# VectorE without two-SBUF-input and copy-mode operations from the first group on; gate rows spread by DMA; split tokens laid by feature chunk; order planned anew

## The chip, the cores and the metric

The kernel runs on one core of one Trainium2 chip, with fp32 inputs. The metric is the device time of one launch in microseconds, as the median of several runs; a profiled execution is taken beside them. PE is TensorE, DVE is VectorE, ACT is ScalarE, POOL is GpSimd and SP is SyncE, which here only issues DMAs. POOL issues DMAs too.

## The reference

One transformer block with adaptive layer norms. `x` has 8 batches of 1024 tokens and 512 features; the six modulation rows of a batch come from `silu(c) @ wmod`.

```python
x = L0_attn_x                                   # 8, 1024, 512
mod = (_silu(L0_c) @ L0_wmod).reshape(8, 6, 1, -1)
sa, ca, ga, sb, cb, gb = (mod[:, i] for i in range(6))
ga = (2 * (ga >= 0) - 1) * jnp.maximum(jnp.abs(ga), 0.25)      # gb likewise
h = _layernorm(x) * (1 + ca) + sa
x = x + ga * attn(h)
h = _layernorm(x) * (1 + cb) + sb
x = x + gb * ffn(h)

# attn: xn = _ln(h, lna_w); q, k, v = projections, 16 heads of 32 features
for it in range(3):
    ql, kl, vl = qcur[:, :, :16] @ Wlq.T + blq, kcur[:, :, :16] @ Wlk.T + blk, vcur[:, :, :16] @ Wlv.T + blv
    t_it = temp0 + 0.005 * it
    tscale = where((t_it != 1.0) & (t_it > 0), rsqrt(t_it), 1.0)
    qs, ks_ = _ln(ql, lnc_w) * tscale, _ln(kl, lnd_w)
    ai = softmax(qs @ ks_.T * sm_scale) @ vl
    iter_out = zeros_like(qcur).at[:, :, :16].set(ai)          # only the first 16 tokens
    diff = mean(abs(iter_out - prev))
    attn_out = where(done, attn_out, iter_out)
    done = done | (diff < thr + fac * diff) & (it > 0)
    prev, qcur, kcur, vcur = iter_out, qcur + iter_out, kl, vl
attn = attn_out @ Wo.T + bo

# ffn: tokens and weight quantized to a 6-bit grid in blocks of 32 features, scale = max(|block|) / 7.5
out = dequantized(x) @ dequantized(weight).T + bias
```

Attention reaches only the first 16 tokens of each batch. For all others `attn` is the row `bo`, so the block's first half adds one gate row `ga * bo` per batch.

## The kernel before

**Groups.** The 1008 tokens per batch outside attention make two groups, one of 4 x 128 and one of 4 x 124 tokens: 16 groups for 8 batches. The 128 attention tokens (16 of each batch) form one tile `xs` of 128 x 512, whose work is spread between the groups from group 2 on.

**One group.** `load(g)`, three groups ahead, brings the tokens with the gate row `ga * bo` added: in mode P SP loads `x` and POOL adds the row `g2B` to each of four tiles (three tiles of group 0 are added on DVE); in mode A ACT copies the row into the tile four times and POOL issues a DMA that adds the tokens to it. `front(g)` normalizes: ACT takes sum and sum of squares with `accum_out`, `rsqrt` runs over ACT, DVE and POOL, and DVE applies two three-operand steps per tile (`A` and `B_`, the modulation rows spread over the partitions, lie in PSUM). DVE reduces the maximum of each block of 32 features (`M`), scales it, and takes the reciprocal `I`. POOL multiplies each tile by `I` into an fp8 tile `q8`, which rounds to the grid, and back by `M` into `x`. PE transposes the tile to `psT`; ACT copies it to `xh` in the reduced format of fp32 that PE multiplies faster, and DVE keeps the remainder `xl = psT - xh`. `back(g)` makes each of four output chunks from 12 matmuls (`xh*wh`, `xh*wl`, `xl*wh`, four feature chunks each) in `psO`; ACT evicts with scale `gbT` and bias `cbT`, POOL issues a DMA that adds the transposed tokens `xT`, and SP stores `outT`. Groups 0 and 1 are cut into parts, the last group is evicted on DVE.

**Gate rows.** `rows(name, src)` takes a 128 x 4 x 8 gate (features on the partitions), writes a negated and a remainder half into `hl`, transposes both and copies 40 rows to SBUF. A matmul with the selector `sel` then spreads a row over the partitions: `make_g2(b)` for the row `g2B` of batch b (copied by ACT from `psT`), `row_s` for RGA and RGB, the gates of the attention tile.

**Attention.** `attc` prepares constants: the two weight matrices centred by their block means (`m2`, `bdc`), the centred biases `rcf`, and the temperature factors `wct`. Three iterations alternate `mix`, `norm`, 32 x 32 transposes, 128 small matmuls for the logits, softmax and 128 small matmuls for the result. After the second, `ds` and `dm` hold whether the iteration had converged; they choose between `ai[1]` and `ai[2]`. Then come the output projection, the gate RGA, the second normalization, quantization, 12 matmuls, the gate RGB and the store `outS`.

**Order.** Every instruction is recorded with a cost and issued in an order that `Program.issue` plans: a list schedule over all engines, whose priorities come from due times per strand (`DUE`, scaled by `LAM`, `MU`, `LAMD`) and from the windows `WP`, `WV`, `WS`, `WE`, `WG` within which an engine is held for a more urgent instruction. The planner has a model of the exclusion between DVE and POOL: `locks` names the instructions concerned, and a locked one starts only when the other engine's current locked instruction is over. Dependences come from `_region`, the span of a tile that an access covers. On the chip each engine, and SP's and POOL's DMA queues, run in exactly the planned order. All instructions are issued through one helper, so that the profile gives them all line 206 and they are told apart by their tiles.

Of the kernel before, what the change touches and what calls it, by code (L numbers as in the profile page):

```python
# [27 lines left out]
LAM = {"gpsimd": 3.714, "scalar": 2.438, "sync": 1.213, "tensor": 0.799, "vector": 5.221}  # L28
MU = 708.0
LAMD = 3.212  # L30
# [3 lines left out]
    "w3": 75770.0,  # L34
    "gb": -217233.0,
    "mod": -252945.0,
    "L0": -248576.0,
    "B0.0": 53715.0,
    "B0.1": 39421.0,
    "B0.2": 59671.0,  # L40
    "B0.3": 62459.0,
    "Q1": -146914.0,
    "B1.0": 75209.0,
    "B1.1": 78188.0,
    "B1.2": 81166.0,
    "B1.3": 84553.0,
    "att0": 32581.0,
    "kv0": 44759.0,
    "it0": 56937.0,
    "kv1": 69216.0,  # L50
    "it1": 81393.0,
    "kv2": 93571.0,
    "it2": 105748.0,
    "end": 152949.0,
    "end2": 165127.0,
    "F2": -150662.0,
    "B2.0": 90191.0,
    "B2.1": 93169.0,
    "B2.2": 96915.0,
    "B2.3": 99126.0,  # L60
    "B3.0": 102005.0,
    "B3.1": 110387.0,
    "B3.2": 107962.0,
    "B3.3": 108731.0,
    "B4.0": 115098.0,
    "B4.1": 118077.0,
    "B4.2": 118615.0,
    "B4.3": 124034.0,
    "B5.0": 123238.0,
    "B5.1": 131709.0,  # L70
    "B5.2": 134688.0,
    "B5.3": 137666.0,
    "L9": -32519.0,
    "B6.0": 142024.0,
    "B6.1": 143731.0,
    "B6.2": 147981.0,
    "B6.3": 150376.0,
    "B7.0": 155080.0,
    "B7.1": 158058.0,
    "B7.2": 154929.0,  # L80
    "B7.3": 164015.0,
    "Q8": 39438.0,
    "B8.0": 168254.0,
    "B8.2": 174211.0,
    "B8.3": 177189.0,
    "F9": 34764.0,
    "B9.0": 162035.0,
    "B9.1": 165249.0,
    "B9.2": 167992.0,
    "B9.3": 172508.0,  # L90
    "B10.0": 193959.0,
    "B10.1": 197581.0,
    "B10.2": 200560.0,
    "B10.3": 203538.0,
    "Q11": 118602.0,
    "B11.0": 207787.0,
    "B11.1": 210766.0,
    "B11.2": 213744.0,
    "B11.3": 216723.0,
    "B12.0": 220952.0,  # L100
    "B12.1": 223986.0,
    "B12.2": 226909.0,
    "B12.3": 229887.0,
    "F13": 142459.0,
    "Q13": 170365.0,
    "B13.0": 234126.0,
    "B13.1": 237105.0,
    "B13.2": 240083.0,
    "B13.3": 243061.0,
    "B14.0": 246786.0,  # L110
    "B14.1": 248083.0,
    "B14.2": 252743.0,
    "B14.3": 255722.0,
    "Q15": 251792.0,
    "B15.0": 260600.0,
    "B15.1": 252121.0,
    "B15.2": 266084.0,
    "B15.3": 269410.0,
# [30 lines left out]
def _region(ap):  # L149

    dims = [tuple(d) for d in ap.ap]
    if ap.space == PSUM:
        return ap.tensor.name, 0, P, 0, 1 << 30
    w = 1
    for s in ap.tensor.shape[1:]:
        w *= s
    p0, f0 = divmod(ap.offset, w)
    np_ = dims[0][1]
    f1 = f0 + sum((n - 1) * abs(s) for s, n in dims[1:]) + 1
    return ap.tensor.name, p0, p0 + np_, f0, f1  # L160
# [9 lines left out]
class Program:  # L170
# [22 lines left out]
    def record(self, name, eng, meth, args, kw):  # L193
# [16 lines left out]
        for ap, wr in [(r, False) for r in reads] + [(w, True) for w in writes]:  # L210
            if ap.space == bass.MemoryType.DRAM:
                continue
            t, a, b, c, d = _region(ap)
            hist = self.acc.get(t, [])
            keep = []
            for h in hist:
                j, w, a2, b2, c2, d2 = h
                over = a < b2 and a2 < b and c < d2 and c2 < d
                if over and (w or wr) and j != i:
                    deps.add(j)  # L220
                if not (wr and a <= a2 and b2 <= b and c <= c2 and d2 <= d):
                    keep.append(h)
            keep.append((i, wr, a, b, c, d))
            self.acc[t] = keep
# [200 lines left out]
def _adaln(ctx: ExitStack, tc: tile.TileContext, t):  # L425
# [11 lines left out]
    WP = 2821  # L437
    WV = 402
    WS = 1017
    WE = 1637  # L440
    WG = 8296
# [27 lines left out]
    xhr = Ring("xh", 2, [P, 4, 4, P], F32R)  # L469
    xlr = Ring("xl", 2, [P, 4, 4, P], F32R)  # L470
# [51 lines left out]
    pkb = new("pkb", [P, 661])  # L522
# [162 lines left out]
    hl = Ring("hl", 2, [P, 4, 40], F32R)  # L685
    for z in hl.tiles:
        G.memset(z.bitcast(F32), 0.0)

    def rows(name, src):

        w = hl()
        V.tensor_scalar(w[:, :, 0:NB], src, -1.0, None, ALU.mult)
        V.scalar_tensor_tensor(w[:, :, 32:40], src, -1.0, w[:, :, 0:NB], ALU.mult, ALU.subtract)
        w = w.bitcast(F32)
        ps = psX()
        for c in range(4):
            PE.transpose(ps[:40, c * P : (c + 1) * P], w[:, c], ident)
        r = new(name, [40, D], F32R)
        S.copy(r, ps[:40])
        return r  # L700

# [13 lines left out]
    def make_g2(b):  # L715
        ps = g2P[b] = psT()
        if b:
            PE.matmul(ps, lhsT=sel[:40, b, :], rhs=Rg2, start=True, stop=True)
        else:
            for c in range(4):  # L720
                PE.matmul(
                    ps[:, c * P : (c + 1) * P],
                    lhsT=g2T[:, c, 0:1].broadcast_to([P, P]),
                    rhs=ident,
                    start=True,
                    stop=True,
                )
        z = g2r()
        S.copy(z, ps)
        g2B[b] = z  # L730
# [3 lines left out]
    Rg2 = rows("Rg2", g2T)  # L734
# [14 lines left out]
    V.tensor_tensor(cbT, gbT, cb(1), ALU.mult)  # L749
    V.tensor_tensor(cbT, cbT, g2T, ALU.add)  # L750
# [52 lines left out]

    def front(g, parts):
# [6 lines left out]
        for js in parts:  # L811
# [30 lines left out]
            V.tensor_scalar(M[:n, : 16 * m], M[:n, : 16 * m], 64.0 / 7.5, 64e-30, ALU.mult, ALU.max)  # L842
            V.reciprocal(I[:n, : 16 * m], M[:n, : 16 * m])
            prog.strand = (g + 1, f"Q{g}")
            for j in js:
# [10 lines left out]
                S.copy(xh[:, j, :, :n], pv)  # L856
                V.tensor_tensor(xl[:, j, :, :n], pv, xh[:, j, :, :n], ALU.subtract)
        return xh, xl

    def back(g, xh, xl, last=False):  # L860
# [14 lines left out]
        for o, j0, m in pieces:  # L875
# [4 lines left out]
            for xs, ws in ((xh, wh), (xh, wl), (xl, wh)):  # L880
                for c in range(4):
                    PE.matmul(ps[:, :M], lhsT=ws[:, o, c, :], rhs=xs[:, j0 : j0 + m, c, :n], start=(i == 0), stop=(i == 11))
# [14 lines left out]
    def attention():  # L897
# [4 lines left out]
        cols, v32, sc = pkb[:, 0:12], pkb[:, 12:18], pkb[:, 18:21]  # L902
        bd = b3(pkb[:, 21:405], P)
        bmask, wk = pkb[:, 405:533], pkb[:, 533:661]
# [17 lines left out]
        V.tensor_scalar(cols[:, 0:4], cols[:, 0:4], qk, None, ALU.mult)  # L922
        V.tensor_scalar(cols[:, 8:12], cols[:, 8:12], -0.5, None, ALU.mult)

        bdc = new("bdc", [P, 2, P])
        m2 = new("m2", [P, 2])
        V.tensor_reduce(m2, bd[:, 0:2], AX.X, ALU.add)
        V.tensor_scalar(m2, m2, 1.0 / 32, None, ALU.mult)
        for i in range(2):
            V.scalar_tensor_tensor(bdc[:, i], bd[:, i], m2[:, i : i + 1], bmask, ALU.subtract, ALU.mult)  # L930
        ps = psX()
        PE.matmul(ps[:, 0:2], lhsT=bmask, rhs=v32[:, 4:6], start=True, stop=True)
        rcf = new("rcf", [P, 2])
        V.scalar_tensor_tensor(rcf, ps[:, 0:2], -1.0 / 32, v32[:, 4:6], ALU.mult, ALU.add)
# [12 lines left out]
        V.scalar_tensor_tensor(wcd, v32[:, 2:3], 0.25, v32[:, 3:4], ALU.mult, ALU.mult)  # L947
# [3 lines left out]
        for i in range(3):  # L951
            V.tensor_scalar(tt[:, i : i + 1], sc[:, 0:1], 0.005 * i, None, ALU.add)
        V.tensor_scalar(tc1, tt, 1.0, None, ALU.not_equal)
        V.scalar_tensor_tensor(tc1, tt, 0.0, tc1, ALU.is_gt, ALU.mult)
        V.tensor_scalar(tt, tt, 1e-30, None, ALU.max)
        rr = rsqrt(tt, P, 3, "t")
        V.scalar_tensor_tensor(tsc, rr, -0.5, tc1, ALU.mult, ALU.mult)
        V.tensor_scalar(tc1, tc1, -1.0, 1.0, ALU.mult, ALU.add)
        V.tensor_tensor(tsc, tsc, tc1, ALU.add)
        V.tensor_scalar(wct, tsc, wcd, None, ALU.mult)  # L960
# [7 lines left out]
        V.tensor_scalar(h1, h1, nm, r, ALU.add, ALU.mult)  # L968
# [82 lines left out]
        ds, dm = new("ds", [P, 1]), new("dm", [P, 1])  # L1051
        qcur = att["WqT"]
        qflat = qcur.rearrange("p a b -> p (a b)")
        for it in range(3):
# [38 lines left out]
            for i0 in range(0, 16, 16 // PARTS):  # L1093
                with prog.together():
                    for i in range(i0, i0 + 16 // PARTS):
                        for h in range(4):
# [8 lines left out]
                            )  # L1105
            a = air()
# [4 lines left out]
            if it == 1:  # L1111
# [6 lines left out]
                V.tensor_scalar(dm, ps[:, 0:1], 1.0 / (NB * 16 * T * 32), None, ALU.mult)  # L1118
                V.scalar_tensor_tensor(ds, dm, sc[:, 2:3], sc[:, 1:2], ALU.mult, ALU.add)
                V.tensor_tensor(dm, dm, ds, ALU.is_lt)  # L1120
                V.tensor_scalar(ds, dm, -1.0, 1.0, ALU.mult, ALU.add)
        prog.strand = ("end", "end")
        V.tensor_scalar(ai[2], ai[2], ds, None, ALU.mult)
        V.scalar_tensor_tensor(ai[2], ai[1], dm, ai[2], ALU.mult, ALU.add)
# [8 lines left out]
        for c in range(4):  # L1133
            PE.matmul(ps, lhsT=ai[2][:, c * P : (c + 1) * P], rhs=w[:, c], start=(c == 0), stop=(c == 3))
        V.tensor_tensor(h1, ps, boP, ALU.add)
        V.tensor_tensor(h1, h1, row_s(rows("RGA", gaT)), ALU.mult)
# [8 lines left out]
        V.tensor_scalar(M, M, 64.0 / 7.5, 64e-30, ALU.mult, ALU.max)  # L1145
# [116 lines left out]
```

## Time and profile before

| | |
|---|---|
| median of 3 runs | 312.61 us (311.56 to 313.08) |
| profiled execution | 310.64 us, its span 308.9 us |
| mean granted PE clock in it | 0.955 |
| DMA | 63.22 MB, mean 205 GB/s |
| POOL's DMA queue | 25.99 MB, 44.8% of the 16 engines' time |
| SP's DMA queue | 36.84 MB, 31.4% |

The busiest groups of each engine, as the page gives them (operation, tile, count, total us, mean ns):

| engine | group | count | us | mean ns |
|---|---|---|---|---|
| PE | MATMUL psO<-xh,wh | 292 | 101.8 | 393 |
| PE | MATMUL psT<-pka,x | 256 | 56.4 | 281 |
| POOL | x<-q,s_M | 64 | 71.9 | 1204 |
| POOL | q<-x,s_I | 64 | 70.3 | 1149 |
| DVE | x<-x,s_nm,psA | 64 | 44.9 | 731 |
| DVE | s_M<-x (maximum) | 19 | 36.8 | 1938 |
| ACT | y<-psO,cbT,gbT | 68 | 49.1 | 723 |
| ACT | x<-g2B | 40 | 22.5 | 625 |

A row's mean is the length of one instruction as the profiler saw it. Matmuls overlap their neighbours, so that the distance between their starts is shorter than their length. A line of a timeline has the start, the length of the merged instructions, engine, operation, output and inputs; what stands in brackets is the idle time before it and the instruction that ended it. The line of 40 digits has one digit for each fortieth of the span, the busy share in tenths; the line PEclk has the granted clock in the same way.

### The profile page before, as it was taken

The numbers are of one execution on the slowest core, as the hardware profiler recorded it, in microseconds if no ns is written. First come the engines' busy times: TensorE is split into PE (matmuls) and PEld (weight loads), VectorE is DVE, ScalarE is ACT, GpSimd is POOL, SyncE is SP. The second block draws the span as 40 slices with busy tenths as digits, with TensorE's granted clock in tenths as the row PEclk, the third lists the DMA queues.
The fourth block names the chain that finished last, engine by engine and source line by source line (L and its number), as shares of the span: only waits on it lengthen the run. The fifth ranks groups of instructions, "written<-read, shape, count | busy, mean of one in ns | idle before, by whom it ended". The sixth has DMA issues, their size and how long they took to land.

```text
span 308.9 us, 6174 instructions
## 1 busy us (share of the span) xinstructions
PE 282.9 (92%) x2235; PEld 216.2 (70%) x2235; DVE 247.2 (80%) x415; ACT 236.6 (77%) x542; POOL 235.4 (76%) x352
## 2 busy tenths in 40 slices
PE   6764999999999999999999995499999999999993
PEld 2332488899797877777778774376788777887783
DVE  6899979998979976968898899959599959961312
ACT  4189889999998998999998979169599979333500
POOL 2779876799998889996999997374999986888010
PEclk9795799999999999999999999589999999999999
DMA  7999947199798697559896829459877977575777
GB/s 247 365 409 388 277 115 232 17 213 209 257 187 261 163 223 180 189 93 230 270 207 186 236 38 213 155 151 191 239 134 261 186 227 138 174 181 129 212 135 270
DMA packets 14846, 63.22 MB, mean 205 GB/s; under 512 B 1630, under 2 KB 2398, under 8 KB 10848
## 3 DMA queue, kind: packets, MB, share of 16 engines
q0 software_dynamic: 3632, 25.99, 44.8%
q1 hardware_dynamic: 11184, 36.84, 31.4%
q8 instruction: 17, 0.28, 0.3%
q14 instruction: 13, 0.11, 0.1%
HBM read 46.05 MB, written 16.78 MB: 203 GB/s over the span
## 4 chain that ended last, share of the span: by engine, by line
PE 57%; DVE 23%; POOL 9%; ACT 5%; issue 3%; DMA 1%; POOLq 0%; DVEq 0%
PE psO L206 39%; PE psX L206 10%; PE psT L206 8%; DVE x L206 7%; DVE s_M L206 5%; POOL x L206 3%; DVE dm L206 3%; POOL q L206 2%; DVE xl L206 2%; ACT jk L206 2%; ACT xh L206 1%; POOL s_u_m L206 1%; PE psA L206 1%; ACT L206 1%; POOL y L206 1%
## 5 line engine op out<-in xcount | busy, mean ns | idle before, releaser
L206 PE MATMUL psO<-xh,wh 128*128 128x512 f32 (+3 forms) x292 | 101.8, 393 | 0.5 <-ACT xh L206 0.5
L206 PE MATMUL psO<-xl,wh 128*128 128x512 f32 (+3 forms) x292 | 99.4, 384 | 0.0
L206 PE MATMUL psO<-xh,wl 128*128 128x512 f32 (+3 forms) x292 | 99.2, 401 | 0.0
L206 POOL TENSOR_TENSOR q<-x,s_I 128x512 fp8e4<-128x512 f32 (+1 forms) x64 | 70.3, 1149 | 16.8 <-DVE s_I L206 5.7
L206 POOL TENSOR_TENSOR x<-q,s_M 128x512 f32<-128x512 fp8e4 (+1 forms) x64 | 71.9, 1204 | 0.1
L206 ACT ACTIVATE y<-psO,cbT,gbT 128x512 f32<-128x512 f32 (+3 forms) x68 | 49.1, 723 | 25.3 <-PE psO L206 25.2
L206 PEld LDWEIGHTS psO<-xh,wh 128*128 128x128 f32 x292 | 53.3, 191 | 17.0 <-ACT xh L206 3.0
L206 PE MATMUL psT<-pka,x 128*128 128x128 f32 (+1 forms) x256 | 56.4, 281 | 8.6 <-DVE xl L206 7.8
L206 PEld LDWEIGHTS psO<-xh,wl 128*128 128x128 f32 x292 | 53.3, 191 | 12.9 <-issue 4.3
L206 PEld LDWEIGHTS psO<-xl,wh 128*128 128x128 f32 x292 | 53.3, 189 | 8.6 <-issue 1.0
L206 DVE TENSOR_TENSOR xl<-psT,xh 128x512 fp32r<-128x512 f32 (+1 forms) x64 | 40.9, 671 | 15.5 <-ACT xh L206 15.5
L206 DVE SCALAR_TENSOR_TENSOR x<-x,s_r_m,psB 128x512 f32<-128x512 f32 (+1 forms) x64 | 43.5, 740 | 10.1 <-POOL s_r_m L206 10.1
L206 DVE SCALAR_TENSOR_TENSOR x<-x,s_nm,psA 128x512 f32<-128x512 f32 (+1 forms) x64 | 44.9, 731 | 5.2 <-PE psA L206 3.5
L206 PEld LDWEIGHTS psT<-pka,x 128*128 128x128 f32 (+1 forms) x256 | 35.2, 145 | 18.1 <-issue 9.9
L206 ACT ACTIVATE jk<-x,s_nm 128x512 bf16<-128x512 f32 (+1 forms) x64 | 46.2, 721 | 0.6
L206 ACT CAST xh<-psT 128x512 fp32r<-128x512 f32 (+1 forms) x64 | 34.4, 577 | 12.3 <-PE psT L206 12.1
L206 ACT ACTIVATE jk<-x 124x512 bf16<-124x512 f32 (+1 forms) x61 | 38.4, 630 | 1.5 <-DMA x<-in_x 1.0
L206 DVE TENSOR_REDUCE s_M<-x 128x64 f32<-128x2048 f32 (+4 forms) x19 | 36.8, 1938 | 0.2
L206 POOL TENSOR_TENSOR x<-x,g2B 124x512 f32<-124x512 f32 (+1 forms) x21 | 27.8, 1389 | 1.7 <-DMA x<-in_x 1.7
L206 ACT COPY x<-g2B 128x512 f32<-128x512 f32 x40 | 22.5, 625 | 0.0
L206 POOL DMA_DIRECT2D y<-in_xT x15 | 13.7, 910 | 11.3 <-ACT y L206 10.9
L206 PE MATMUL psX<-ai,w 128*128 128x128 f32 x96 | 15.5, 275 | 0.0
(236 smaller groups left out, 376.8 us busy)
## 6 DMA issues: line engine op xcount, KB each, us to landing
x<-in_x POOLq DMA_DIRECT2D x10, 1024.0 KB, 10.4
y<-in_xT POOLq DMA_DIRECT2D x8, 1024.0 KB, 8.2
outT<-y SPq DMA_DIRECT2D x8, 1024.0 KB, 7.3
y<-in_xT POOLq DMA_DIRECT2D x7, 992.0 KB, 7.9
outT<-y SPq DMA_DIRECT2D x7, 992.0 KB, 4.1
x<-in_x SPq DMA_DIRECT2D x5, 1024.0 KB, 6.9
y<-in_wmod SPq DMA_DIRECT2D x16, 256.0 KB, 5.9
x<-in_wmod SPq DMA_DIRECT2D x8, 256.0 KB, 7.3
```

Source lines behind the costliest of these rows:

```text
L206: o.fn = lambda: getattr(eng, meth)(*args, **kw)
```

## The change

Four things change together.

1. From the first group on, DVE has no more instructions that read two SBUF operands or that run from SBUF to SBUF as a scaling or a copy. They go to POOL (the scaling of `M`, `cbT`, the constants of attention, two products with RGA and RGB), to ACT (the normalized `h1`, and the product of `ai[1]` with `dm`), to PE (the centred weights), or read one operand from PSUM (`dm`, `ds`, the last choice between the iterations). Three tiles of group 0 are still added on DVE.
2. `rows` writes 8 plain fp32 rows. `make_g2(b)` for b > 0 and the gates RGA and RGB of the attention tile are spread by DMAs on SP's queue instead of matmuls.
3. For groups 2 to 15 `xh` and `xl` are laid out with the feature chunk outermost and the group's 4n tokens in one run; groups 0 and 1 keep one block per tile of 128 tokens. `_region` learns of the columns within a period of 512.
4. The planner's due times and weights are other ones, so the order of all instructions is another.

The diff, with the two tables of due times left out and repeated renamings shortened:

```diff
-LAM = {"gpsimd": 3.714, "scalar": 2.438, "sync": 1.213, "tensor": 0.799, "vector": 5.221}
-MU = 708.0
-LAMD = 3.212
+LAM = {"gpsimd": 3.429, "scalar": 3.529, "sync": 0.785, "tensor": 0.578, "vector": 5.271}
+MU = 650.1
+LAMD = 2.969
...
-    WP = 2821
-    WV = 402
-    WS = 1017
-    WE = 1637
-    WG = 8296
+    WP = 4984
+    WV = 0
+    WS = 223
+    WE = 189
+    WG = 24984
...
-    xhr = Ring("xh", 2, [P, 4, 4, P], F32R)
-    xlr = Ring("xl", 2, [P, 4, 4, P], F32R)
+    xhr = Ring("xh", 2, [P, 4 * D], F32R)
+    xlr = Ring("xl", 2, [P, 4 * D], F32R)
...
-    def rows(name, src):
-
-        w = hl()
-        V.tensor_scalar(w[:, :, 0:NB], src, -1.0, None, ALU.mult)
-        V.scalar_tensor_tensor(w[:, :, 32:40], src, -1.0, w[:, :, 0:NB], ALU.mult, ALU.subtract)
-        w = w.bitcast(F32)
+    rw = new("rw", [96, D])
+
+    def rows(i, src):
+        r = rw[32 * i : 32 * i + NB]
         ps = psX()
         for c in range(4):
-            PE.transpose(ps[:40, c * P : (c + 1) * P], w[:, c], ident)
-        r = new(name, [40, D], F32R)
-        S.copy(r, ps[:40])
+            PE.transpose(ps[:NB, c * P : (c + 1) * P], src[:, c], ident)
+        S.copy(r, ps[:NB])
         return r
+
+    def spread(r, z):
+
+        for b in range(NB):
+            SY.dma_start(z[16 * b : 16 * b + 16], r[b : b + 1].unsqueeze(1).broadcast_to([1, 16, D]))
+        return z
...
     def make_g2(b):
+        z = g2B[b] = g2r()
+        if b:
+            SY.dma_start(z, Rg2[b : b + 1].unsqueeze(1).broadcast_to([1, P, D]))
+            return
         ps = g2P[b] = psT()
-        if b:
-            PE.matmul(ps, lhsT=sel[:40, b, :], rhs=Rg2, start=True, stop=True)
...
-    V.tensor_tensor(cbT, gbT, cb(1), ALU.mult)
-    V.tensor_tensor(cbT, cbT, g2T, ALU.add)
+    G.tensor_tensor(cbT, gbT, cb(1), ALU.mult)
+    G.tensor_tensor(cbT, cbT, g2T, ALU.add)
...
+    def by_tile(z, g):
+        return z.rearrange("p (j c k) -> p j c k", j=4, c=4)
+
+    def by_chunk(z, g):
+        n = GR[g][2]
+        return z.rearrange("p (c k) -> p c k", c=4)[:, :, : 4 * n]
+
+    def part(z, g, j):
+        n = GR[g][2]
+        return by_tile(z, g)[:, j, :, :n] if g < 2 else by_chunk(z, g)[:, :, j * n : j * n + n]
+
+    def moving(z, g, c, j0, m):
+        n = GR[g][2]
+        return by_tile(z, g)[:, j0 : j0 + m, c, :n] if g < 2 else by_chunk(z, g)[:, c, j0 * n : (j0 + m) * n]
...
-            V.tensor_scalar(M[:n, : 16 * m], M[:n, : 16 * m], 64.0 / 7.5, 64e-30, ALU.mult, ALU.max)
+            G.tensor_scalar(M[:n, : 16 * m], M[:n, : 16 * m], 64.0 / 7.5, 64e-30, ALU.mult, ALU.max)
...
-                S.copy(xh[:, j, :, :n], pv)
-                V.tensor_tensor(xl[:, j, :, :n], pv, xh[:, j, :, :n], ALU.subtract)
+                h, l = part(xh, g, j), part(xl, g, j)
+                S.copy(h, pv)
+                V.tensor_tensor(l, pv, h, ALU.subtract)
...
-                    PE.matmul(ps[:, :M], lhsT=ws[:, o, c, :], rhs=xs[:, j0 : j0 + m, c, :n], start=(i == 0), stop=(i == 11))
+                    PE.matmul(ps[:, :M], lhsT=ws[:, o, c, :], rhs=moving(xs, g, c, j0, m), start=(i == 0), stop=(i == 11))
...
-        V.tensor_reduce(m2, bd[:, 0:2], AX.X, ALU.add)
-        V.tensor_scalar(m2, m2, 1.0 / 32, None, ALU.mult)
-        for i in range(2):
-            V.scalar_tensor_tensor(bdc[:, i], bd[:, i], m2[:, i : i + 1], bmask, ALU.subtract, ALU.mult)
+        bdf = new("bdc", [P, 2 * P + 2])
+        bdc, rcf = b3(bdf[:, : 2 * P], P), bdf[:, 2 * P :]
         ps = psX()
-        PE.matmul(ps[:, 0:2], lhsT=bmask, rhs=v32[:, 4:6], start=True, stop=True)
-        rcf = new("rcf", [P, 2])
-        V.scalar_tensor_tensor(rcf, ps[:, 0:2], -1.0 / 32, v32[:, 4:6], ALU.mult, ALU.add)
+        PE.matmul(ps[:, :P], lhsT=wq, rhs=cen, start=True, stop=True)
+        PE.matmul(ps[:, P : 2 * P], lhsT=wk, rhs=cen, start=True, stop=True)
+        PE.matmul(ps[:, 2 * P : 2 * P + 2], lhsT=cen, rhs=v32[:, 4:6], start=True, stop=True)
+        V.tensor_copy(bdf, ps[:, : 2 * P + 2])
...
-        V.tensor_scalar(h1, h1, nm, r, ALU.add, ALU.mult)
+        nr = new("nr", [P, 1])
+        G.tensor_tensor(nr, nm, r, ALU.mult)
+        S.activation(h1, h1, AF.Identity, scale=r, bias=nr)
...
+            if it == 2:
+                V.scalar_tensor_tensor(ai[1], av, ds, ai[1], ALU.mult, ALU.add)
+                break
             a = air()
             S.copy(a, av)
...
-                V.tensor_scalar(dm, ps[:, 0:1], 1.0 / (NB * 16 * T * 32), None, ALU.mult)
-                V.scalar_tensor_tensor(ds, dm, sc[:, 2:3], sc[:, 1:2], ALU.mult, ALU.add)
-                V.tensor_tensor(dm, dm, ds, ALU.is_lt)
-                V.tensor_scalar(ds, dm, -1.0, 1.0, ALU.mult, ALU.add)
+                V.tensor_scalar(ps[:, 1:2], ps[:, 0:1], 1.0 / (NB * 16 * T * 32), None, ALU.mult)
+                V.tensor_scalar(dt_, ps[:, 1:2], sc[:, 2:3], sc[:, 1:2], ALU.mult, ALU.add)
+                V.tensor_tensor(dm, ps[:, 1:2], dt_, ALU.is_lt)
+                V.tensor_tensor(ds, ps[:, 1:2], dt_, ALU.is_lt)
+                G.tensor_scalar(ds, ds, -1.0, 1.0, ALU.mult, ALU.add)
+
+                S.mul(a, a, dm)
...
-        V.tensor_scalar(ai[2], ai[2], ds, None, ALU.mult)
-        V.scalar_tensor_tensor(ai[2], ai[1], dm, ai[2], ALU.mult, ALU.add)
...
-        V.tensor_tensor(h1, h1, row_s(rows("RGA", gaT)), ALU.mult)
+        G.tensor_tensor(h1, h1, spread(rows(1, gaT), new("RGA", [P, D])), ALU.mult)
...
-        V.tensor_scalar(M, M, 64.0 / 7.5, 64e-30, ALU.mult, ALU.max)
+        G.tensor_scalar(M, M, 64.0 / 7.5, 64e-30, ALU.mult, ALU.max)
...
-        V.tensor_tensor(h1, h1, row_s(rows("RGB", gbT)), ALU.mult)
+        G.tensor_tensor(h1, h1, spread(rows(2, gbT), new("RGB", [P, D])), ALU.mult)
```

The twelve small steps that make `cols`, `wcd`, `tt`, `tsc`, `tc1` and `wct` move from DVE to POOL in the same way; the packed constants `pkb` grow from 661 to 792 columns, with the iteration offsets, the centring matrix and the transposed weights.

## The prediction

> **What bounds the kernel now.** I read the busy shares first, then the slices, then the list of waits, and last the timeline around the longest wait.
>
> ```profile
> span 308.9 us, 6174 instructions
> ...
> PE 282.9 (92%) x2235; PEld 216.2 (70%) x2235; DVE 247.2 (80%) x415; ACT 236.6 (77%) x542; POOL 235.4 (76%) x352
> ...
> PE   6764999999999999999999995499999999999993
> ...
> PEclk9795799999999999999999999589999999999999
> ```
>
> TensorE (PE) is busy in every slice but the first four, two between 185 and 201 us and the last; its granted clock drops near 200 us too. From 60 to 180 us it works 119.5 of 120 us at full clock, while the windows view gives ACT 112.6, POOL 109.5 and VectorE (DVE) 103.2: they feed PE with little to spare. So the time is PE's work, plus its idle stretches, plus what it loses at a lowered clock. The list of waits names the longest idle stretch:
>
> ```profile
> PE psT L206 <- DVE xl L206: 7.8, 2, 7.4
> ```
>
> The timelines of DVE, of POOL and of PE there:
>
> ```profile
> 181.51 0.69 DVE L206 TENSOR_TENSOR t<-psX,s_mx 128x512 f32<-128x512 f32 x1
> 182.11 8.85 DVE L206 TENSOR_TENSOR dm<-dm,ds 128x1 f32<-128x1 f32 x1
> 190.88 2.71 DVE L206 SCALAR_TENSOR_TENSOR x<-x,s_r_m,psB 128x512 f32<-128x512 f32 x4
> ```
>
> ```profile
> 184.48 1.54 POOL L206 TENSOR_TENSOR x<-x,g2B 124x512 f32<-124x512 f32 x1
> 185.71 1.14 POOL L206 DMA_DIRECT2D x<-in_x  x1
> 186.32 2.62 POOL L206 TENSOR_TENSOR q<-x,s_I 124x512 fp8e4<-124x512 f32 x2
> 188.34 2.59 POOL L206 TENSOR_TENSOR x<-q,s_M 124x512 f32<-124x512 fp8e4 x2
> 197.97 1.05 POOL L206 TENSOR_TENSOR t<-t,s_mx 128x512 f32<-128x512 f32 x1 [7.04 <-DVE s_M L206]
> ```
>
> ```profile
> 188.76 1.07 PE L206 MATMUL psO<-xl,wh 128*128 128x512 f32 x4
> 197.24 1.06 PE L206 MATMUL psT<-pka,x 124*128 124x124 f32 x4 [7.41 <-DVE xl L206]
> ```
>
> A comparison of one element per partition, with both inputs in SBUF, takes 8.85 us and ends within 0.1 us of the moment at which POOL runs out of work (188.34 + 2.59 = 190.93). Behind it in DVE's order stand the second normalization of four tiles, their maxima and two low halves `xl` that free the transposes' PSUM, so PE idles 7.41 us. The windows behind the gap (PE busy, PEld, DVE, ACT, POOL, then the granted clock):
>
> ```profile
> 195.00:200.00 5.00, 2.77 (x10) 2.31 (x11) 4.93 (x10) 1.28 (x3) 1.93 (x2) 0.50 0.29 119
> 200.00:205.00 5.00, 5.00 (x141) 3.68 (x140) 3.06 (x6) 2.15 (x3) 4.45 (x8) 0.72 0.47 164
> ```
>
> 2.77 us of work at 0.50 lose 1.4 us, 5.00 at 0.72 lose 1.4: the stall costs PE 7.4 + 2.8 = 10.2 us. Afterwards PE is busy to the end, with ACT, DVE and POOL well under full from 260 us on, so it is not won back.
>
> That this is a class of instruction and not one accident, two rows of the scale tile show:
>
> ```profile
> L206 DVE TENSOR_SCALAR s_M<-s_M x19: 132/189/1229, 26.2 to 274.6; 128x64 f32<-128x64 f32 x7, 124x64 f32<-124x64 f32 x7, 128x16 f32<-128x16 f32 x2, 124x32 f32<-124x32 f32 x2
> L206 DVE RECIPROCAL s_I<-s_M x19: 189/541/554, 27.5 to 274.8; 128x64 f32<-128x64 f32 x7, 124x64 f32<-124x64 f32 x7, 128x16 f32<-128x16 f32 x2, 124x32 f32<-124x32 f32 x2
> ```
>
> The first form stretches ninefold (132 to 1229 ns), the reciprocal of the same tile never does.
>
> [...]
>
> **The change, part by part** (against the profiled execution: 310.64 us, span 308.9).
>
> *1. The port stalls.* `dm` and its twin `ds` now read PSUM and SBUF, as the 0.69 us subtraction above does with no stretch; the 2.23 us multiplication of `ai` and the 0.75 us step behind it become one step from PSUM (about 0.74, by the 734 ns of a three-operand row with a PSUM input). All 10.2 us of PE could return. But ACT at 94% and POOL at 91% between 60 and 180 us have to feed PE without that pause, so some of it comes back as short waits. Taken: -9; bounds -10.2 and -3.
>
> *2. PE's own work.* Seven `g2B` matmuls and the two that spread RGA and RGB go (nine; the chain shows 0.44 us for the one of RGA, rows mean 498 to 539 ns): 9 x 0.44 = 4.0. New are two 128-column f32 products and a two-column one, at most 3 x 0.28 (row of 128-column transposes) = 0.8. Taken: -3; bounds -4.5 (9 x 0.5, nothing added on the path) and 0.
>
> *3. The start.* Between 14 and 47 us the chain runs through DVE, which is busy 10.0 of the 10 us from 20 on. Off DVE go `cbT` (1.72 + 0.19), two scalings of `s_M` (1.30), two of `hl` (0.53 + 1.03), and the constants' sums and centred weights (0.40 + 0.16 + 0.34 x 2); of these the chain holds about 3.7 us (1.69, 0.15, some 1.2 of the `s_M` pieces, 0.32, 0.23, 0.12). In exchange each of the first parts sends its maximum through POOL: 0.35 us (POOL's 128x16 TENSOR_SCALAR, 353 ns) plus two hand-overs of about 0.1 to 0.2 us. Two on the chain give back 1.2. Taken: -2; bounds -4 and +1 (if each stands behind one POOL product of 1.2 us more).
>
> *4. Contiguous tokens.* The moving operand of groups 2 to 15 becomes one run. The last stretch shows four-run steps of 512 columns every 0.23 us (286.15, 286.38, 286.61); a contiguous 512 product, `psA`, also takes 0.23 on the chain. Taken: 0. Bound -2: 336 products of 496 columns now also step by about 0.23, and would by proportion step by 0.222, so 6 ns each. A slower read is excluded by the contiguous row.
>
> *5. POOL's load.* Added: 20 scalings, 14 of 64 elements at about 0.4 (between 353 ns for 16 and 1202 for 512 elements) and 6 smaller ones at 0.3, two products `h1` at 1.30 (row `xs<-xs,h`), some sixteen tiny ones at 0.2 to 0.35: 5.6 + 1.8 + 2.6 + 4.5 = about 14 us, POOL 235 to 250. DVE loses about 30 us (9.0 of `s_M` and `s_sM`, 8.7, 2.2, 1.9, 2.8, 1.9 of `h1`, 3.5 of constants), ACT about 3 (seven copies of 576 ns and one of `ai` go, two near 0.7 come). Most of it lies in POOL's idle time, but a scaling on POOL now stands between DVE's reduction and DVE's reciprocal. Taken: +2; bounds 0 and the second rival.
>
> *6. Gate rows by DMA.* Seven broadcasts of 256 KB and sixteen small ones enter SP's queue, 0.33 to 0.4 us of issue each, 9 us of a queue that mostly waits. Behind a waiting broadcast on SP stand the `outT` stores that free `y`, and the `x` loads. The trace has no copy from one partition to 128. Nearest are the broadcasts of `bo` and `bias` from DRAM, 11.0 and 4.6 us to landing; loads are issued three groups ahead, and 14 groups take from about 75 us to the end, some 15 us each. Taken: 0; bounds 0 and the first rival. [...]
>
> *7. The new order.* Nothing shows what it is worth; it carries the width, 6 us to either side.
>
> Sum: -9 - 3 - 2 + 0 + 2 = -12, so 298.6. The median of the runs lies 2.0 above the profiled execution (312.61 to 310.64): 300.6, rounded to **300**. All gains at their best: -20.7, or 292 as a median, 290 with a little of part 7.
>
> **Rivals.**
> - *Late gate rows.* SP takes its queue in order and has waited up to 15.5 us for one `y` transfer; a broadcast behind it comes late. ACT then stops in the four copies `x<-g2B`, and with it the evictions of `psO`, of which PE has two. Five groups load in this way (2, 4, 6, 10, 12); at 2 us of PE each, 10 us: **310.5**. Against it: three groups of lead.
> - *POOL's queue takes the place of the lock (slower).* Place: the scaling of each group's maximum, in order on POOL behind `q` and `x` products, which run back to back. If each of 14 groups waits one product and two hand-overs that PE sees, 14 x (1.2 + 0.3) = 21 us, against gains of 14: 310.6 + 7 + 2 = **319.5**. It decides from (14 + 1.6)/14 = 1.1 us per group on. For it: POOL at 91%, and `psT` weights already wait 9.7 us on `s_M`'s products. Against it: two `xh` buffers, and DVE, 30 us lighter, reduces earlier.
> - *The stall survives elsewhere.* [...] Then only parts 2 to 5 remain, -3: **309.5**. Against it: no reduction, transpose, reciprocal or PSUM-fed form shows a stretch.
>
> **How the numbers follow.** Forecast 0.62, late rows 0.12, POOL's queue 0.16, surviving stall 0.10. A measurement of this kernel tells about 0.5% from no change, so faster is below 311.0 and slower above 314.2. Faster: 0.62, plus 0.06 of the late rows and 0.06 of the surviving stall; same: 0.07; slower: 0.16 and 0.03 of the late rows. The forecast's own range is 292 to 307; to leave no more than 2 in 10 out it reaches over both middle rivals, to 290 and 314.
>
> **What would show it.** No DVE instruction over 2.5 us after 40 us; PE without a gap over 2 us after 60 us and with the clock at 1.00 there; no PE group from `Rg`; POOL near 250 us, DVE near 217. Wrong: a new wait of DVE's reciprocal on POOL, or of ACT's copies on the broadcasts, that adds up to 10 us of idle PE; or PE slices below 9 between 60 and 280 us.

## The result: 11% slower, and the profile after

The changed kernel takes 347.27 us (346.0 to 348.33) against 312.09 us for the kernel before in the same rounds: a ratio of 1.1122 [1.1067, 1.1177]. Forecast were 300 us, 290 to 314. The direction was wrong. (Of the experiments below, the profiled execution of the one with ACT's queue was disturbed; its page is used there, its time is not.)

The first lines of the page of the changed kernel: busy time per engine, the slices, the granted clock, the DMA engines.

```profile
span 344.9 us, 6191 instructions
...
PE 287.4 (83%) x2230; PEld 220.8 (64%) x2230; DVE 223.1 (65%) x366; ACT 233.9 (68%) x536; POOL 248.4 (72%) x389
...
PE   6872989719998864999499999459999999999992
...
PEclk9875789976999896999999999959999999999998
DMA  7999999993499996298999479996749979478596
```

DVE and POOL have come out as forecast (223 for 217, 248 for 250). But PE's row of nines is now broken in five places between the first slices and the last. Idle PE is the span less its busy time: 26.0 us before (308.9 - 282.9), 57.5 now, so 31.5 of the 36.0 us are new holes. The other 4.5 are PE's own work, longer although instructions went: the mean granted clock fell from 0.955 to 0.917, and the digits of the clock are low at most of the holes or just behind them.

What the holes wait for, from the list of waits (us in all, times, longest):

```profile
PEld psO L215 <- ACT y L215: 24.4, 11, 9.0
PE psO L215 <- ACT y L215: 21.5, 7, 8.3
ACT y L215 <- DMA outT<-y: 13.0, 3, 6.0
ACT jk L215 <- DMA x<-in_x: 18.3, 4, 7.1
ACT x L215 <- DMA g2B<-rw: 2.7, 1, 2.7
```

PE waits for evictions. ACT, which makes them, waits for `outT` stores to free a `y` buffer and for loads of `x`. The gate rows themselves delay ACT by 2.7 us once. So the culprit isn't the row that comes late; it is something that makes other transfers late. The hole at 219.6 us shows what. Timelines of SP, ACT and PE:

```profile
206.16 0.48 SPq L215 DMA_DIRECT2D g2B<-rw  x1
207.44 24.04 SPq L215 DMA_DIRECT2D outT<-y  x2
```

```profile
227.06 0.78 ACT L215 ACTIVATE y<-psO,cbT,gbT 128x512 f32<-128x512 f32 x1 [5.57 <-DMA outT<-y]
```

```profile
227.89 0.80 PE L215 MATMUL psO<-xh,wh 128*128 128x512 f32 x1 [8.33 <-ACT y L215]
```

The chain of waits names the same transfer: the `outT` issued at 207.44 takes 19.52 us, where no `outT` before took over 9.5. (Such a time runs from the issue of a DMA until all its bytes have landed.)

```profile
207.44 19.52 DMA outT<-y
```

Beside it lies the broadcast issued at 206.16, which landed after 15.2 us. The view of the DMAs from 200 to 232 us, in 40 slices of 0.8 us, shows the DMA engines' busy share and what they moved:

```profile
DMA  4897997998899979987988967999999898999985
GB/s 51 102 164 164 215 276 164 195 256 174 174 236 202 148 125 72 49 28 23 28 26 23 36 115 284 425 410 272 189 248 199 189 270 183 204 256 204 194 184 122
```

From the 18th to the 22nd slice the 16 engines are busy for 70% of the time or more and move only 23 to 28 GB/s. The trace records a transfer in packets. A packet of the broadcast (2 KB, one partition's row) takes 1.08 us; the median 2 KB packet of the kernel before took 84 ns (packet times are read from the packed traces, no view lists them). One broadcast has 128 of them. The page has the sum by queue (packets, MB, share of the 16 engines' span):

```profile
q1 hardware_dynamic: 12704, 39.27, 43.8%
q0 software_dynamic: 3632, 25.99, 38.5%
```

SP's queue held the engines for 43.8% of 344.9 = 151 us; before for 31.4% of 308.9 = 97. Only 2.4 MB were added. Their landings, and what lay beside them (us to landing):

```profile
x<-in_x POOLq DMA_DIRECT2D x10, 1024.0 KB, 16.7
...
g2B<-rw SPq DMA_DIRECT2D x7, 256.0 KB, 13.0
```

Loads on POOL's own queue went from 10.4 to 16.7 us, so it is not SP's order alone. The other transfers' packets are not slower in themselves: beside the broadcast issued at 151.56 us POOL's 8 KB packets take 628 ns at the median, as they did before (629), but only 23 of them get through in 11 us, although a load of 128 had been issued at 152.12. Between 153.55 and 161.88 us not one packet of POOL's queue begins, while up to 16 of the broadcast's are in flight at once. My reading is that they wait for a turn on engines that the broadcast holds; the experiments test it.

### The profile page after: what moved, and what is told of

Read it like the earlier page. It is cut to its first block, busy times and chain, and to the rows that moved or that the text cites. A ratio compares the mean times of both kernels' runs of the same rounds, so it can differ in the third digit from the quotient of the medians.

```text
span 344.9 us, 6191 instructions
## 1 busy us (share of the span) xinstructions
PE 287.4 (83%) x2230; PEld 220.8 (64%) x2230; DVE 223.1 (65%) x366; ACT 233.9 (68%) x536; POOL 248.4 (72%) x389
## 3 DMA queue, kind: packets, MB, share of 16 engines
q1 hardware_dynamic: 12704, 39.27, 43.8%
## 4 chain that ended last, share of the span: by engine, by line
PE 43%; DMA 33%; ACT 10%; POOL 5%; DVE 4%; issue 2%; SPq 0%; ACTq 0%; POOLq 0%
PE psO L215 32%; DMA outT<-y 16%; DMA x<-in_x 8%; DMA y<-in_xT 7%; PE psX L215 6%; PE psT L215 5%; ACT jk L215 3%; ACT y L215 2%; POOL x L215 2%; ACT x L215 2%; DVE x L215 1%; POOL q L215 1%; ACT xh L215 1%; DMA w<-in_w 1%; DVE wr L215 1%
## 5 line engine op out<-in xcount | busy, mean ns | idle before, releaser
L215 PE MATMUL psO<-xh,wh 128*128 128x512 f32 (+3 forms) x292 | 108.4, 416 | 23.2 <-ACT y L215 21.5
L215 PE MATMUL psO<-xl,wh 128*128 128x512 f32 (+3 forms) x292 | 103.0, 396 | 2.2 <-issue 2.2
L215 PE MATMUL psO<-xh,wl 128*128 128x512 f32 (+3 forms) x292 | 104.0, 406 | 0.0
L215 PEld LDWEIGHTS psO<-xh,wh 128*128 128x128 f32 x292 | 56.8, 206 | 40.7 <-ACT y L215 24.4
L215 POOL TENSOR_TENSOR x<-q,s_M 128x512 f32<-128x512 fp8e4 (+1 forms) x64 | 68.6, 1106 | 0.2
L215 PE MATMUL psT<-pka,x 128*128 128x128 f32 (+1 forms) x256 | 61.0, 278 | 7.8 <-POOL x L215 7.1
L215 PEld LDWEIGHTS psO<-xh,wl 128*128 128x128 f32 x292 | 54.8, 196 | 11.1 <-issue 2.2
L215 DVE SCALAR_TENSOR_TENSOR x<-x,s_r_m,psB 128x512 f32<-128x512 f32 (+1 forms) x64 | 43.8, 736 | 9.0 <-POOL s_r_m L215 9.0
L215 PEld LDWEIGHTS psT<-pka,x 128*128 128x128 f32 (+1 forms) x256 | 36.2, 144 | 16.0 <-POOL x L215 8.0
L215 POOL TENSOR_TENSOR x<-x,g2B 124x512 f32<-124x512 f32 (+1 forms) x21 | 27.5, 1378 | 12.6 <-DMA x<-in_x 8.3
L215 DVE RECIPROCAL s_I<-s_M 128x64 f32<-128x64 f32 (+4 forms) x19 | 9.1, 481 | 14.6 <-POOL s_M L215 14.6
## 6 DMA issues: line engine op xcount, KB each, us to landing
x<-in_x POOLq DMA_DIRECT2D x10, 1024.0 KB, 16.7
```

Source lines behind the costliest of these rows:

```text
L215: o.fn = lambda: getattr(eng, meth)(*args, **kw)
```

## The experiments

Theories, with the letters that some expectations use: **A**, the broadcasts. **A1**: their source is one partition, the packets are slow, and the 16 shared engines are taken from all others. **A2**: it is their bytes and places in SP's queue as such. **A3**: they merely stand in SP's queue ahead of `outT`. Against A: the new order (**B**), or POOL's heavier load (**C**). On the gain that was forecast: **S**, the stalls of DVE behind POOL are worth what PE lost beside them; **S2**, the work behind them only meets the next limit. Later, on what makes a packet slow: **P**, groups of four neighbouring partitions share a limited path; **Q**, it is the single partition. All ratios are against the kernel before run beside them (311.35 to 311.7 us).

### The kernel before with the broadcasts alone

```diff
     def make_g2(b):
-            PE.matmul(ps, lhsT=sel[:40, b, :], rhs=Rg2, start=True, stop=True)
+            SY.dma_start(z, Rg2[b : b + 1].unsqueeze(1).broadcast_to([1, P, D]))
+            return
...
-    Rg2 = rows("Rg2", g2T)
+    Rg2 = new("rw", [NB, D])
...
```

> The kernel before, with only the seven gate rows spread by DMA from one partition of plain fp32 rows. Theory A: 330 to 350 us, packets of 2 KB near 1.1 us, other transfers beside a broadcast at 14 us or more. Theories B and C: 310 to 314 us, since nothing else of the change is in it.

337.01 us, ratio 1.0825 [1.0768, 1.0883]. The packets take 1.08 us here too, a broadcast 12.6 us to its landing, and idle PE is 333.9 - 283.4 = 50.5 us for 26.0.

```profile
g2B<-rw SPq DMA_DIRECT2D x7, 256.0 KB, 12.6
```

The due times and weights are those of before, and nothing has moved to POOL. The planner, given fewer instructions, made another order, though, so this run by itself does not part the broadcasts from the order. Its new waits are those of the changed kernel: the one below was 1.0 us before, and the longest `outT` takes 18.4 us for 9.5. The broadcasts, with the order made around them, cost 8%.

```profile
ACT jk L206 <- DMA x<-in_x: 17.3, 3, 8.1
```

### The changed kernel with 16 source partitions

The same bytes by the same DMAs on the same queue, in nearly the same order; but each row lies in 16 neighbouring partitions, each of which is read 8 times.

```diff
-            SY.dma_start(z, Rg2[b : b + 1].unsqueeze(1).broadcast_to([1, P, D]))
+            SY.dma_start(z, Rg2[16 * b : 16 * b + 16].unsqueeze(1).broadcast_to([16, 8, D]))
...
-    Rg2 = rows(0, g2T)
+    Rg2, rep = new("rg", [P, D]), new("rep", [P, D])
+    S.copy(b3(rep, 16), g2T.rearrange("p a b -> p (a b)").unsqueeze(2).broadcast_to([P, 4 * NB, 16]))
+    ps = psX()
+    for c in range(4):
+        PE.transpose(ps[:, c * P : (c + 1) * P], rep[:, c * P : (c + 1) * P], ident)
+    S.copy(Rg2, ps)
```

> The changed kernel, with each gate row first replicated in 16 partitions (an ACT copy, four transposes, a copy) and the DMA reading it from those 16, each 8 times: the same bytes, packets and queue. If the single source partition is what makes the packets slow (A1), they fall from 1.08 us to below 0.4 and the time to 300 to 318 us. If it is the extra bytes and places in SP's queue as such (A2), the time stays at 335 us or more.

**307.93 us, ratio 0.9878 [0.985, 0.9906]**: the whole loss is gone, and a little more.

```profile
span 306.7 us, 6192 instructions
...
PE 278.9 (91%) x2230; PEld 215.3 (70%) x2230; DVE 222.9 (73%) x366; ACT 233.6 (76%) x537; POOL 247.2 (81%) x389
...
q1 hardware_dynamic: 12704, 39.27, 39.2%
...
x<-in_x POOLq DMA_DIRECT2D x10, 1024.0 KB, 11.7
...
g2B<-rg SPq DMA_DIRECT2D x7, 256.0 KB, 5.6
```

As many packets and bytes on SP's queue as in the changed kernel, but a packet takes 0.295 us, and the `x` loads are back at 11.7 us. Of the 38.2 us of span that this gives, 29.7 are idle PE (57.5 to 27.8) and 8.5 are PE busy (287.4 to 278.9) at a better clock (0.957). How late the changed kernel's `psO` products start, against this one's, by the time in this one:

```
at us      46    52    72    102   120   150   188   198   end
late us  +0.6  +4.4 +12.3 +17.1 +22.9 +27.9 +28.0 +39.1 +37.8
```

It rises in steps, and these lie beside the broadcasts or just behind them (issued at 43.6, 90.6, 111.1, 151.6 and 206.2 on the changed kernel's clock).

### The broadcasts on ACT's queue

```diff
-            SY.dma_start(z, Rg2[b : b + 1].unsqueeze(1).broadcast_to([1, P, D]))
+            src = Rg2[b : b + 1].unsqueeze(1).broadcast_to([1, P, D])
+            SY.dma_start(z, src)
+            prog.ops[-1].fn = [lambda: nc.scalar.dma_start(z, src)]
```

> The changed kernel, order unchanged, with the seven broadcasts from one partition issued by ACT instead of SP, so that no outT or x transfer stands behind them in SP's queue. If the harm is the queue's order (A3), 325 us or less. If the slow packets hold the DMA engines that all queues share (A1), 335 us or more, with POOL's transfers still near 17 us beside a broadcast.

351.6 us in one execution. Packets 1.07 us, ACT's four waits for `outT` 21.5 us in all, and on the page of the profiled execution:

```profile
x<-in_x POOLq DMA_DIRECT2D x10, 1024.0 KB, 18.2
...
g2B<-rw ACTq DMA_DIRECT2D x7, 256.0 KB, 13.1
```

Another queue does not help, and A3 falls: beside broadcasts on ACT's queue the loads on POOL's take 18.2 us, as beside those on SP's (16.7; before 10.4).

### The old due times and weights

The due times and weights of the kernel before, in the changed kernel and in the one with 16 source partitions.

```diff
-MU = 650.1
+MU = 708.0
...
-    WP = 4984
+    WP = 2821
...
```

> The changed kernel with the due times, weights and windows of the planner as before. Theory A: 330 us or more, since the broadcasts remain. Theory B: 300 to 314 us.

> The kernel with gate rows read from 16 partitions, planned with the due times, weights and windows of before. If the new plan carries a gain of its own (B reversed), 311 us or more; if the order hardly matters, 305 to 310 us; if the new plan costs, 304 us or less.

355.62 us, ratio 1.1423 [1.1391, 1.1455], and 318.87 us, ratio 1.0244 [1.0196, 1.0292]. The order is not the cause: for this code the new plan is 8 us (to 347.27) or 11 us (to 307.93) better than the old one, which was made for other instructions.

### Gate rows by matmul, in the changed kernel

```diff
-        if b:
-            SY.dma_start(z, Rg2[b : b + 1].unsqueeze(1).broadcast_to([1, P, D]))
-            return
...
-                lhsT=g2T[:, c, 0:1].broadcast_to([P, P]),
+                lhsT=g2T[:, c, b : b + 1].broadcast_to([P, P]),
```

> The changed kernel, with every gate row g2B again spread by four 128-column matmuls and an ACT copy instead of a DMA; the rest of the change (VectorE's instructions, layout, due times, RGA and RGB by DMA) stays. If the broadcasts from one partition hold up the DMA engines (theory A), the gaps of PE shrink from 49 to below 25 us and the time comes to 300 to 312 us. If the new order is what costs (theory B), or the scaling on POOL (theory C), it stays at 335 us or more.

331.44 us, ratio 1.062 [1.0564, 1.0676]: a miss. The broadcasts of `g2B` are gone, `x` loads (mean 8.4 us) and `outT` (4.9) are quick, and yet PE idles 38.6 us (330.2 - 291.6). The planner, given other instructions under the new due times, made a widely different order of ACT and PE. Two things changed at once. Against the kernel with 16 source partitions PE is busy 12.7 us longer and idle 10.8 us longer; how much of that the order does and how much the added PE and ACT work was not separated. Order and added work together can thus cost this kernel more than 20 us; so the runs that keep an order, or nearly so, carry the argument.

### How a packet's time goes with the source

With 16 partitions spaced by 8 instead of neighbouring, and with four neighbours read 32 times each:

```diff
-            SY.dma_start(z, Rg2[16 * b : 16 * b + 16].unsqueeze(1).broadcast_to([16, 8, D]))
+            SY.dma_start(z, Rg2[b :: NB].unsqueeze(1).broadcast_to([16, 8, D]))
```

> As the kernel with 16 source partitions (307.9 us), order unchanged, but the 16 partitions lie 8 apart (b, b+8, ...) instead of side by side. If neighbouring partitions share a way to the DMA engines (P: port groups), the broadcast's packets fall from 293 ns to below 200 and the time by 0 to 3 us, to 305 to 308. If each partition has its own limit (Q), the packets stay at 270 to 310 ns and the time at 307 to 309 us.

```diff
-            SY.dma_start(z, Rg2[16 * b : 16 * b + 16].unsqueeze(1).broadcast_to([16, 8, D]))
+            SY.dma_start(z, Rg2[16 * b : 16 * b + 4].unsqueeze(1).broadcast_to([4, 32, D]))
```

> As the kernel with 16 source partitions, order unchanged, but each gate row is read from the first 4 of its 16 partitions, each 32 times. P (four neighbours share one way): packets near 1.08 us again and 335 us or more, as from one partition. Q (a limit per partition): packets of 0.3 to 0.6 us and 308 to 320 us.

Spaced: 308.16 us, ratio 0.9829 [0.9777, 0.988], as with neighbours. Four: **405.57 us, ratio 1.3028 [1.2988, 1.3068]**, which is P's side (335 or more), but far worse than from one partition. All three kernels with copied rows issue the same instructions in the same order. A packet of 2 KB, the DMA engines at work on a broadcast at once (16 at the most; fewer at its start and end), and the rate that follows while so many are at work (engines x 2048 B / packet time):

```
source partitions      packet ns   engines   GB/s
1                           1080        16     30
4 neighbours            290-1200      3.5-4  28 to 7
16 neighbours                295        16    111
16, spaced by 8              158        16    207
```

Four neighbours give at best about what one partition gives (28 GB/s and 30), and 16 neighbours, four groups of four, give four times that (111). So neighbours share a limited path. That is P, and a limit for each partition (Q) is out, though the packets of the four came out nearer to Q's figure, with 3.5 to 4 engines at work on them and not 16. The source spaced by 8 touches sixteen groups of four and yet gives only 207 GB/s, 13 for each group, so the group of four is not the whole rule. What else limits that source, and whether the path is a port, as the name in the expectation has it, no run shows. Why the packets of the four neighbours take up to 1.2 us in some stretches stays open.

With four source partitions the transfer was worked on by some 3.5 engines at a time, so 128 packets lasted until 25 to 45 us after the issue. Why it was so few was not shown. The waits show the price:

```profile
PEld psO L215 <- ACT y L215: 64.2, 9, 22.2
ACT y L215 <- DMA outT<-y: 63.2, 3, 22.5
PE psO L215 <- ACT y L215: 62.0, 6, 21.9
```

ACT waits up to 22.5 us for one `outT`. What holds it so long was not shown.

### `dm` alone

What was the stall worth by which the forecast lived? The kernel before, in its own order, with the one comparison issued on POOL.

```diff
                 V.tensor_tensor(dm, dm, ds, ALU.is_lt)
+                prog.ops[-1].fn = [lambda: nc.gpsimd.tensor_scalar(dm, dm, ds, None, ALU.is_lt)]
```

> The kernel before with its order unchanged; only the comparison dm moves from VectorE to POOL, at the same place of the order. If the stall of 8.85 us is worth what PE lost beside it (theory S, prediction's part 1), the gap of 7.4 us on PE falls below 2 us and the time to 301 to 305 us. If the work behind it only meets the next limit (theory S2: POOL and ACT cannot feed PE faster), the gap shrinks or moves and the time stays at 307 us or above.

307.51 us for 311.35, ratio 0.986 [0.9813, 0.9907], -3.8 us by the medians and -4.4 by the ratio; in the profiled executions the span goes from 308.9 to 302.9. The lines of POOL and PE that answer to those of before:

```profile
183.25 0.49 POOL L1121 TENSOR_SCALAR dm<-dm,ds 128x1 f32<-128x1 f32 x1
```

```profile
190.99 0.64 PE L206 MATMUL psT<-pka,x 124*128 124x124 f32 x4 [0.44 <-POOL x L206]
```

8.85 us have become 0.49, PE's gap of 7.41 has become 0.44. Against the kernel before the products run 0.8 us late until 184 us, then 5.9 early, and so to the end. The stall was there and was not won back, as the forecast had it; its size in this order was 4 to 6 us, not 9.

### The scaling on DVE or on POOL

The 16-partition kernel with the 19 scalings of `M` issued on DVE again, at their places:

```diff
-            G.tensor_scalar(M[:n, : 16 * m], M[:n, : 16 * m], 64.0 / 7.5, 64e-30, ALU.mult, ALU.max)
+            Mv = M[:n, : 16 * m]
+            G.tensor_scalar(Mv, Mv, 64.0 / 7.5, 64e-30, ALU.mult, ALU.max)
+            prog.ops[-1].fn = [lambda v=Mv: nc.vector.tensor_scalar(v, v, 64.0 / 7.5, 64e-30, ALU.mult, ALU.max)]
```

> The kernel with gate rows read from 16 partitions (307.9 us), its order unchanged; the 19 scalings of s_M of the groups go back to VectorE at their places. If the scaling on POOL stands in the chain (theory C), it becomes 2 us or more faster, 306 or less, and VectorE's waits for s_M on POOL (9.6 us) go. If the port stalls come back and count (theory S), some scaling takes over 1 us and the time rises to 309 or more. If neither matters for PE, 307 to 309 us.

308.03 us, ratio 0.9882 [0.9842, 0.9922], the same as with POOL (307.93). The stretches are back (min, median and longest in ns) and cost nothing there:

```profile
L873 DVE TENSOR_SCALAR s_M<-s_M x19: 171/194/2833, 28.0 to 267.4; 128x64 f32<-128x64 f32 x7, 124x64 f32<-124x64 f32 x7, 128x16 f32<-128x16 f32 x2, 124x32 f32<-124x32 f32 x2
```

The kernel before, in its own order, with the scalings, `cbT` and `dm` issued on POOL and the product of `ai` on ACT; and the same with these 19 scalings left on DVE (the attention tile's own stays on POOL):

```diff
-            V.tensor_scalar(M[:n, : 16 * m], M[:n, : 16 * m], 64.0 / 7.5, 64e-30, ALU.mult, ALU.max)
+            Mv = M[:n, : 16 * m]
+            V.tensor_scalar(Mv, Mv, 64.0 / 7.5, 64e-30, ALU.mult, ALU.max)
+            prog.ops[-1].fn = [lambda v=Mv: nc.gpsimd.tensor_scalar(v, v, 64.0 / 7.5, 64e-30, ALU.mult, ALU.max)]
...
         V.tensor_scalar(ai[2], ai[2], ds, None, ALU.mult)
+        prog.ops[-1].fn = [lambda: nc.scalar.mul(ai[2], ai[2], ds)]
```

> The kernel before with its order, layout and gate rows unchanged; at their places of the order, the scalings of s_M, s_sM, cbT and dm go from VectorE to POOL and the product of ai with ds to ACT. Theory S (port stalls are the gain): no VectorE instruction over 1.5 us after 40 us, and 302 to 306 us, at least as fast as dm alone (307.5). If POOL's extra load (C) costs what the stalls gave, 308 us or more.

> As the kernel before with dm, cbT, s_sM and the ai product moved at their places, but the 19 scalings of s_M stay on VectorE. If these scalings on POOL are what ate the gain in that order (theory C), 303 to 308 us, no slower than dm alone (307.5). If the other moves did it, 310 to 312 us as with all moved.

311.02 us, ratio 0.9981 [0.995, 1.0012], for 302 to 306 expected, a miss; and 307.26 us, ratio 0.9869 [0.9841, 0.9898]. With the scalings moved no DVE instruction but the reductions (2.28 us) takes over 1.4 us after 40 us, and yet the gain is gone: the products are 4.7 us late by 184, at most 3.9 early behind the stall, 0.4 early by 207 and 0.4 late at the end. Of its waits the first line below was 10.1 before, and the second is new:

```profile
DVE x L206 <- POOL s_r_m L206: 15.0, 9, 3.0
DVE s_I L206 <- POOL s_M L846: 9.6, 10, 1.5
```

Without the scalings the second line is absent, the first falls to 11.8, and the lead of 5.8 us by 207 lasts to the end (5.4). So in the order of before the scalings on POOL cost 3.8 us (311.02 - 307.26); in the new order, planned with them in place, nothing.

## Why the prediction was wrong, step by step

**The step that failed is part 6, gate rows by DMA**, "Taken: 0; bounds 0 and the first rival". It asked when the row arrives, and three groups of lead answered that: ACT waited 2.7 us for a row in all. It did not ask what the transfer holds up on its way. With 16 source partitions in place of one, at the same bytes, queue and near enough the same order, 39 us go (347.27 to 307.93); in the kernel before, the broadcasts and the order made around them cost 25 us (311.7 to 337.01). The two rows it went by landed after 11.0 and 4.6 us; the broadcasts took 11 to 15, once 28.1. What it left out is that the engines are shared: the packets of a source that gives 30 GB/s sat in up to 16 of them at once, and beside the broadcast issued at 151.56 us no packet of POOL's queue began for 8.3 us. SP's queue held the engines 54 us longer than before (151 for 97). Even without this loss the sum is 8 us too low (307.93 for 300), and parts 1 and 3 below are the terms that came out smaller than taken. Those two rows, broadcasts from DRAM, do not have a single partition as their source.

**The rival "Late gate rows"** had the right part of the change and the wrong mechanism. Its price, 10 us, was set by ACT's copies; the cost came through `outT`, `x` and `y` transfers beside the broadcast.

**Part 1, the port stalls (-9).** No run shows a port; they show the stretch and its price. `dm` takes 8.85 us in the kernel before and 157 ns in the changed one, and with `dm` alone moved PE's gap goes from 7.41 us to 0.44. The size was -3.8 by the medians, -6.0 in the profiled spans. That is within the bounds, and it is a single instruction's worth.

**Part 2, PE's own work (-3).** PE busy goes from 282.9 to 278.9 in the 16-partition kernel, with the clock nearly equal (0.955, 0.957), and no `Rg` group is left. It agrees with the term but was not isolated.

**Part 3, the start (-2).** Not there. PE's busy time in windows, kernel before, then 16 source partitions (first column after the length of the window):

```profile
20.00:40.00 20.00, 13.84 (x95) 8.40 (x96) 19.27 (x44) 18.61 (x48) 18.74 (x36) 0.66 1.04 343
40.00:80.00 40.00, 39.26 (x298) 35.31 (x298) 36.03 (x71) 37.92 (x102) 32.14 (x55) 1.00 0.68 162
...
180.00:220.00 40.00, 32.59 (x325) 24.21 (x311) 33.38 (x39) 27.32 (x59) 26.15 (x35) 0.87 0.71 162
```

```profile
20.00:40.00 20.00, 10.79 (x80) 6.63 (x79) 17.34 (x37) 18.20 (x50) 18.15 (x44) 0.66 0.98 303
40.00:80.00 40.00, 35.56 (x271) 31.34 (x270) 28.98 (x47) 36.23 (x96) 33.34 (x56) 1.00 0.73 180
...
180.00:220.00 40.00, 39.60 (x312) 30.38 (x311) 32.97 (x53) 36.60 (x80) 39.13 (x58) 1.00 0.88 219
```

PE gets 7.0 us more work done from 180 to 220 us, where the stall was, and 6.8 us less from 20 to 80 us. The one gain is nearly all taken back by the other loss; that goes with a repaired kernel 1.2% and not 4% below the kernel before. Which of the moved instructions or of the new order holds PE up there was not tried.

**Part 4, contiguous tokens (0, bound -2).** Consecutive products of 496 columns start 224 ns apart (median) for 228 before; 336 x 4 ns is 1.3 us, inside the bound.

**Part 5 and the rival "POOL's queue".** DVE's reciprocal waits 14.6 us on POOL's scaling in the changed kernel, as the rival said. In the kernel with 16 source partitions, where this wait is 9.6 us, it costs nothing by the run with the scalings back on DVE. In the order of before it costs 3.8 us, a little more than the +2 taken and far from 21.

**Part 7, the new order (6 to either side).** Against the old due times and weights it is worth 8 to 11 us for the changed code; what an order made as well for the old code would be worth stays open.

**The rival "The stall survives elsewhere"** is out: after 40 us neither `dm` (157 ns) nor any other moved form stretches (the scalings on POOL take 283 to 459 ns).

Five versions beat the changed kernel clearly and the kernel before by a little, all near 307 to 308 us: the changed one with 16 source partitions, neighbouring, spaced, or with the scalings back on DVE, and the kernel before with `dm` on POOL, alone or with the constants moved too. They can't be told apart, and the last two need no new order. All versions of the changed kernel still spread RGA and RGB from one partition by sixteen small DMAs; those of RGB take 1.0 us per packet and hold the engines for 6.6 us near the end. What that costs was not tried.

## What to carry to other kernels

Price a transfer by the time that it keeps the shared DMA engines, packets x packet time / 16 (here 128 x 1.08 / 16, an estimated 8.6 us a broadcast), not by its own landing, and ask which buffers the transfers beside it free. A row to be spread by DMA should lie in 16 partitions first, neighbouring or spaced by 8: a copy, four transposes and a copy did that here and were worth 39 us; four partitions made it worse (405.57 us). Removing a stall from one engine pays only if the work is not put in front of another engine's queue (in the order of before 307.26 us with the scalings left on DVE, 311.02 with them on POOL); try the one costly instruction alone first.

## What the runs showed of the hardware that was not expected

- A DMA read from one SBUF partition took 1.08 us per 2 KB packet on each of 16 engines, about 30 GB/s in all; `outT` stores and `x` loads on the same queue grew from at most 9.5 and 9.1 us to 19.5 and 28.2, `x` loads on POOL's queue from at most 12.2 to 20.0.
- Four source partitions instead of one made it worse (405.57 us for 347.27): the work sat on about four engines for 25 to 45 us, and ACT waited 63.2 us in three waits for `outT` stores.
- A DVE comparison of one element per partition took 8.85 us, through eight compute instructions of POOL, and ended within 0.1 us of the last; as an instruction of POOL it took 0.49 us. The other stretches of this class, up to 2.83 us, cost nothing measurable in the new order (308.03 us with the scalings on DVE, 307.93 on POOL).
